# Moving read-outs, gates, norms and TensorE groups in the schedule of two state-space layers

## The chip, the core and the metric

The kernel runs on one core of a Trainium2 chip. That core has five engines which work side by side, each through its own instructions in order: TensorE (PE, matmuls; PEld is its weight load), VectorE (DVE), ScalarE (ACT), GpSimd (POOL) and SyncE (SP), which here only issues DMA transfers. They wait for one another by semaphores. The metric is the device time of one launch in microseconds (us), lower is better. Before the change the median of three runs is 9307.3 us (9303.51 to 9308.01).

## The reference

The network takes `x` of 8 images, 384 channels, 32 x 32 pixels, in float32, and applies four layers, each as `x = x + layer(group_norm(x))`:

- Layer 0 is a Mamba block over the 1024 pixels of an image as a sequence.
- Layer 1 is a deformable depthwise convolution with three kernel sizes.
- Layer 2 is a layer norm, the same state-space block, and an MLP with exact gelu.
- Layer 3 shifts channel groups and convolves them.

The change touches layers 0 and 2. Their common core, cut to what matters (768 inner channels `d`, 16 states `n`, sequence `t`):

```python
xz = t @ in_proj_w.T;  xm, z = split(xz)
u  = silu(causal_conv3(xm) + conv_b)
dt, B, C = split(u @ x_proj_w.T)
dt = softplus(dt @ dt_proj_w.T + dt_proj_b)
h[t] = exp(dt * A) * h[t-1] + (dt * u) * B[t]      # for every d and n
y[t] = sum_n h[t] * C[t] + u * D
out  = (y * silu(z)) @ out_proj_w.T
# layer 2 alone: out = gelu(out @ mlp_w1.T) @ mlp_w2.T, after a layer norm in front
```

## The kernel before

Each state-space layer is one call of `ssm_layer` (L205). The sequence of an image is cut into two halves of 512 tokens, so there are 16 **steps** a layer (8 images x 2 halves). Counting from 0, an even step is the first half of an image and an odd step the second. The 768 inner channels are six tiles `j` of 128.

A tile has 8 **units** `m`. A unit is one scan instruction: 128 partitions hold 32 channels x 4 states, and the free dimension holds two further states of 512 tokens each, so 128 x 1024 elements. A step has 6 x 8 = 48 units, which the code counts as slots `t` 0 to 47. For each unit:

- `decays` (L490, ACT): `da = exp(dt * A)`, two instructions, into one of two PSUM buffers, two units ahead.
- `inputs` (L498, POOL): `db = du * B`, three units ahead, with three buffers.
- `scan` (L508, DVE): the recurrence, one instruction over `da` and `db`.
- `with_c` (L522): `hs = h * C`, on POOL for some units (`GP_C`: those scan straight into `hs`) and on DVE for the others. There are seven `hs` buffers.
- `keep_last` (L517, ACT): in the first half the last state is kept for the second; `first_token`, `carry` and `add_carry` (L463 to L487) put it in there.
- `read_out` (L530, PE): after each four units, 8 matmuls (16 rows in the trace, since each float32 matmul shows as two passes) add `hs` over the states into `y`, a single PSUM buffer. In layer 0 the first of the two read-outs of a tile begins with a matmul that adds `u * D`.

After the second read-out of a tile `close` (L553, DVE) multiplies `y` by the gate `silu(z)`.

Everything else is hung into this row of units by `plan` (L652). It fills four lists, for ACT, DVE, POOL and PE, with one entry per slot; `put(q, t, fn, ...)` adds a function to slot `t`. The order on each of these four engines is exactly the order in which the loop at L782 emits it (`tc.manual_schedule`), so a wait of one instruction holds up all that follow on its engine. Within a unit the order is: ACT's list, scan and its product, `keep_last`, `decays` of two units ahead, DVE's list, `inputs` of three ahead, POOL's product, POOL's list, PE's list, and then the read-outs kept in `late`. Read-outs kept in `early` are emitted at the beginning of a unit. SP's transfers are ordered by the framework, not by hand.

What `plan` places, with the slots that the change touches:

- the gates: `fetch_in` and `z_proj` (L542, PE) and `gate` (L548, ACT). Silu, gelu and the pair exp/ln lie in different ACT tables, so each gate is a table load, the silu, and by `exp_ln` (L376) a load back;
- the softplus of tile `j + 2`: `dt_proj` (PE), `soft_exp` (ACT), `soft_rest` (DVE, writes `sp_e`), `soft_ln` (ACT), and then in layer 0 `soft_add` (L441, PE: three matmuls by the identity into `ps_sp`), `soft_take` (L446, ACT) and `soft_du` (L449, DVE), and in layer 2 `soft_sum` (L432, POOL). `spread` (L453, SP) writes `dt` and `du` to DRAM and reads them back spread over the partitions as `dtb` and `dub`;
- the next step's input: `norm_load`, in odd steps the group norm of the next image (`gn_...`), `norm_apply`, in layer 2 the layer norm (`ln_mean` to `ln_affine`), the six inner projections with their convolution (`inner`, `conv_last`, `conv`, `silu`), `x_proj`, `x_store`, `load_bc`;
- the previous step's output: `out_proj` (L564), `out_take`, and in layer 2 the MLP in three groups (`mlp_up`, `up_take`, `gelu`, `mlp_down`, `down_take`), whose weights come through a ring of three buffers `wm`.

All these matmuls share three PSUM banks (`mm`), used in turn.

## Time and profile before

| | us |
|---|---|
| median of the runs | 9307.3 |
| profiled execution | 9306.84 |
| its span | 9305.0 |
| layer 0, 75 to 2902 of the span | 2827 |
| layer 1, 2902 to 5863 | 2961 |
| layer 2, 5863 to 8996 | 3133 |
| rest (tail of the MLP, layer 3), 8996 to 9305 | 309 |
| one unit's scan on DVE, mean | 2.28 to 2.29 |
| its product on DVE (where it has one) | 1.225 |
| `db` product on POOL | 2.356 |
| `hs` product on POOL (where it has one) | 2.354 |
| one decay on ACT (two a unit) | 0.691 |
| ACT table load | 1.283 |
| gate (silu of 128 x 512) on ACT | 0.597 |
| gelu of 128 x 2048 on ACT | 1.910 |
| six 128 x 128 x 512 matmul passes on PE | 2.74 |

How to read it: the span is the time from the first to the last instruction of the profiled execution. A stretch of the span can be asked for alone, and then shows how long each engine was busy in it. The list of waits says which instruction (engine, tile, line) waited for which, with the sum in us, the number of times and the longest. A timeline row gives start, duration, engine, line, operation, tiles and shapes, and in brackets the idle time of that engine just before it and what ended it. In the timelines of this document, times are us from the start of the span.

### The profile page before, as it was taken

What the parts mean: (1) busy time and instruction counts of PE and PEld (TensorE: products, weight loads), DVE (VectorE), ACT (ScalarE), POOL (GpSimd) and SP (SyncE); (2) the same over time, 40 slices, a digit from 0 to 9 for tenths busy, and PEclk for the clock granted to TensorE, in tenths of its full rate; (3) what the DMA queues carried; (4) which work ended last, traced back from release to release, by engine and by line L of the source; (5) the groups of instructions that cost most, each with busy time, mean ns of one, the idle gap of its engine ahead of it and who ended that gap; (6) DMA issues with size and microseconds to landing.
All of it is one profiled execution on the core that took longest, in us unless ns stands there. A gap on an engine that the chain in (4) does not pass through costs nothing. (4 is left out here: it accounts for less than half of the span.)

```text
span 9305.0 us, 93009 instructions
## 1 busy us (share of the span) xinstructions
PE 7688.2 (83%) x29427; PEld 3852.5 (41%) x29452; DVE 7740.8 (83%) x8617; ACT 6580.6 (71%) x10531; POOL 5646.0 (61%) x3393
## 2 busy tenths in 40 slices
PE   6777777777775999999999997588888888888886
PEld 2222222222222777777777776133333333333333
DVE  6999999999995778778878877788989889898973
ACT  5677677677674778778878877677777777777750
POOL 6999999999995000000000000798989989899964
PEclk8888888888887999999999998798999899999988
DMA  4444544544443333333333333466656666565656
GB/s 126 119 117 112 122 118 114 123 115 113 120 110 88 77 82 86 90 84 88 89 80 88 89 83 86 115 152 150 150 146 148 156 158 153 145 147 147 162 147 112
DMA packets 785232, 1094.48 MB, mean 118 GB/s; under 512 B 274962, under 2 KB 427954, under 8 KB 752984
## 3 DMA queue, kind: packets, MB, share of 16 engines
q1 hardware_dynamic: 722628, 1077.98, 47.3%
q10 hardware_dynamic: 62100, 10.44, 0.7%
q8 instruction: 236, 3.87, 0.2%
q14 instruction: 268, 2.20, 0.1%
HBM read 917.84 MB, written 170.33 MB: 117 GB/s over the span
## 5 line engine op out<-in xcount | busy, mean ns | idle before, releaser
L502 POOL TENSOR_TENSOR db<-dub,bc 128x1024 f32<-128x1024 f32 x1536 | 3604.3, 2356 | 381.3 <-DVE hs L514 183.9
L494 ACT ACTIVATE da<-dtb,vec 128x512 f32<-128x512 f32 x3072 | 2118.6, 691 | 622.0 <-DVE hs L527 356.8
L514 DVE TENSOR_TENSOR_SCAN da<-da,db 128x1024 f32<-128x1024 f32 x912 | 2087.2, 2289 | 268.7 <-ACT da L494 205.5
L435 POOL TENSOR_TENSOR dt<-dt,sp_e 128x512 f32<-128x512 f32 x96 | 122.5, 1276 | 2893.2 <-DVE sp_e L427 2893.2
L1597 PE MATMUL wacc<-fsm,fxk 128*128 128x221 f32 (+34 forms) x10624 | 1657.0, 315 | 96.4 <-DVE fsm L1567 94.0
L537 PE MATMUL y<-hs,cols 128*32 128x512 f32 x6144 | 1170.6, 710 | 631.9 <-POOL hs L525 554.3
L1597 PEld LDWEIGHTS wacc<-fsm,fxk 128*128 128x128 f32 x10624 | 1570.3, 195 | 234.5 <-DVE fsm L1567 157.8
L514 DVE TENSOR_TENSOR_SCAN hs<-da,db 128x1024 f32<-128x1024 f32 x624 | 1423.3, 2281 | 90.9 <-POOL db L487 60.9
L525 POOL TENSOR_TENSOR hs<-hs,bc 128x1024 f32<-128x1024 f32 x624 | 1468.6, 2354 | 32.8 <-ACT st L520 32.8
L1567 DVE TENSOR_TENSOR fsm<-fhy,fhx 128x170 f32<-128x170 f32 (+42 forms) x3216 | 1172.9, 434 | 345.3 <-PE wacc L1597 318.4
L527 DVE TENSOR_TENSOR hs<-da,bc 128x1024 f32<-128x1024 f32 x912 | 1117.0, 1225 | 78.8 <-PE y L537 23.3
L1527 ACT ACTIVATE fhy<-fpyx,cell 128x416 f32<-128x416 f32 (+9 forms) x1280 | 645.5, 576 | 388.1 <-DVE fsm L1567 388.1
L537 PEld LDWEIGHTS y<-hs,cols 128*32 128x32 f32 x6144 | 219.7, 119 | 1472.9 <-POOL hs L525 800.5
L1550 DVE TENSOR_TENSOR fxk<-fxt,fwk 128x1024 f32<-128x1024 f32 (+1 forms) x688 | 789.0, 1185 | 10.2 <-ACT fxt L1329 10.2
L614 PE MATMUL ps_m<-hid,wm 128*128 128x512 f32 x1152 | 608.8, 686 | 145.8 <-ACT hid L609 91.0
L595 PE MATMUL ps_h<-t,wm 128*128 128x512 f32 x1152 | 524.7, 599 | 24.5 <-DVE sp_e L427 15.0
L1532 ACT ACTIVATE fhy<-fhy,cols 128x1344 f32<-128x1344 f32 (+10 forms) x368 | 530.8, 1442 | 12.0
L614 PEld LDWEIGHTS ps_m<-hid,wm 128*128 128x128 f32 x1152 | 247.4, 222 | 511.8 <-issue 291.6
L1238 PE MATMUL ps_off<-fxn,fow 128*98 128x465 f32 (+10 forms) x896 | 386.6, 579 | 0.0
L1514 ACT ACTIVATE fhx<-fpyx,cell 128x544 f32<-128x544 f32 (+8 forms) x640 | 380.0, 666 | 0.0
L595 PEld LDWEIGHTS ps_h<-t,wm 128*128 128x128 f32 x1152 | 214.0, 190 | 322.6 <-issue 276.1
L569 PE MATMUL ps_o<-u,wm 128*128 128x512 f32 x576 | 292.1, 655 | 64.1 <-DMA wm<-in_wout 38.8
(212 smaller groups left out, 9969.6 us busy)
## 6 DMA issues: line engine op xcount, KB each, us to landing
dtb<-dtd SPq DMA_DIRECT2D x768, 256.0 KB
dub<-dtd SPq DMA_DIRECT2D x768, 256.0 KB
fpyx<-fposd SPq DMA_DIRECT2D x640, 256.0 KB
wm<-in_w SPq DMA_DIRECT2D x96, 768.0 KB
bc<-bcd SPq DMA_DIRECT2D x256, 256.0 KB
x<-x SPq DMA_DIRECT2D x71, 768.0 KB
dtd<-dt SPq DMA_DIRECT2D x192, 256.0 KB
dtd<-du SPq DMA_DIRECT2D x192, 256.0 KB
```

The source lines that it names most:

```text
L494: nc.scalar.activation(da[:, i, :], s["dtb", j][:, k, :], AF.Exp, scale=na[:, j, n + i : n + i + 1])
L502: nc.gpsimd.tensor_tensor(db, du, s["bc"][p][:, 0], ALU.mult)
L514: nc.vector.tensor_tensor_scan(h1, da1, db1, 0.0, ALU.mult, ALU.add)
L525: nc.gpsimd.tensor_tensor(s["hs", m], s["hs", m], c, ALU.mult)
L527: nc.vector.tensor_tensor(hs_tile(s, m), s["da", m], c, ALU.mult)
L537: nc.tensor.matmul(s["y"][k * IP : (k + 1) * IP, :], sel, s["hs", p * NSUB + k][:, i, :], start=mlp and p == 0 and i == 0, stop=p == NQP - ...
L595: nc.tensor.matmul(ps, s["w1", q][:, k, f * P : (f + 1) * P], s["t"][:, k, :], start=(k == 0), stop=(k == G - 1))
L614: nc.tensor.matmul(ps, s["w2", q][:, f, o * P : (o + 1) * P], s["hid", q][:, f, :], start=(f == 0), stop=(f == 3))
L1527: nc.scalar.activation(hy[:, at : at + (yb - ya) * W], pyx[:, 0, ya * W : yb * W], AF.Abs, bias=bias)
L1550: nc.vector.tensor_tensor(t[:, :n], x, wk[:, j : j + 1, :].to_broadcast([P, n, P]), ALU.mult)
L1567: nc.vector.tensor_tensor(self.sub(sm, at, [(r * w, n), (w, r), (1, w)]), self.sub(hy, hy_at[by] + xa, [(r * W, n), (W, r), (1, w)]), self ...
L1597: nc.tensor.matmul(a[:, ya - 4 * o : yb - 4 * o, xa:xb], k, self.sub(sm, sm_at[by], [(w, yb - ya), (1, w)]), start=False, stop=False,)
```

## The change

Eight edits, all in `ssm_layer`, with no instruction added to the arithmetic:

1. `du` no longer has a tile of its own; it is written into `sp_e` (the tile that `soft_rest` wrote). `sz` gets two buffers in layer 2.
2. Read-outs: the first of a tile (units 0 to 3) goes from the end of slot 4 to the end of slot 5; the second (units 4 to 7) from the beginning of the next tile's first unit to the end of that unit, behind PE's list. `early` disappears.
3. `close` goes from slot 1 to slot 2 of the next tile.
4. In layer 0 `soft_du` goes from slot 6 to slot 7 of the tile.
5. In layer 2 the gates of tiles 0 and 1 share one table visit at slot 8, those of 2 and 3 one at slot 24; the others come at 31 and 47 (before: 7, 15, 23, 31, 39, 47). The z projections move with them. Layer 0 keeps its slots.
6. The group norm's last parts (`gn_sum`, `gn_rstd`) and `norm_apply` go one slot later, the parts of the layer norm one or two.
7. In layer 2 the first three inner projections, `x_proj` and `x_store` go one or two slots later.
8. In layer 2 the halves of `out_proj`, and the groups of `mlp_up`, `mlp_down` and gelu, get new slots (gelu 17, 33, 42 becomes 15, 33, 41).

```diff
-                s["du", j] = du = p1.tile([P, TS], F32, name="du")
+                s["du", j] = du = s["e"]
...
             def gate(s, j):
-                sz = s["sz"] = p1.tile([P, TS], F32, name="sz")
-                nc.scalar.activation(sz, s["ps_z"], AF.Silu)
+                sz = s["sz", j] = p1.tile([P, TS], F32, name="sz", bufs=2 if mlp else 1)
+                nc.scalar.activation(sz, s["ps_z", j], AF.Silu)
...
+            TG, TS2 = ((8, 8, 24, 24, 31, 47), (24, 31)) if mlp else ((7, 15, 23, 31, 39, 47), (23, 31))
+            TZ = (6, 7, 22, 23, 30, 45) if mlp else tuple(t - 1 for t in TG)
+            TI = (16, 17, 18, 24, 25, 26) if mlp else (15, 16, 17, 24, 25, 26)
...
-                    put(dve, t + 1, close, *((s, j - 1) if j else (prev, ND - 1)))
-                    tz = t + (6 if pe_sum or mlp and j == 0 else 5)
+                    put(dve, t + 2, close, *((s, j - 1) if j else (prev, ND - 1)))
+                    tz = TZ[j]
                     put(pe, tz - 2, fetch_in, s, ND + j)
                     put(pe, tz, z_proj, s, j)
-                    g = t + 7
-                    put(act, g, gate, s, j)
-                    if j in (2, 3):
-                        put(act, g, silu, nxt, 3 * (j - 2), 3 * (j - 1))
-                    put(act, g, exp_ln)
+                    put(act, TG[j], gate, s, j)
...
-                        put(dve, t + 6, soft_du, n, k)
+                        put(dve, t + 7, soft_du, n, k)
...
+                for i, t in enumerate(TS2):
+                    put(act, t, silu, nxt, 3 * i, 3 * i + 3)
+                for t in sorted({*TG, *TS2}):
+                    put(act, t, exp_ln)
...
-                    put(dve, 7, lambda n: n.update(gn_var=self.gn_sum(n["gn_grp"][0], n["gn_ps"])), nxt)
-                    put(act, 8, lambda n: n.update(gn=self.gn_rstd(n["gn_grp"][0], n["gn_var"])), nxt)
+                    put(dve, 8, lambda n: n.update(gn_var=self.gn_sum(n["gn_grp"][0], n["gn_ps"])), nxt)
+                    put(act, 9, lambda n: n.update(gn=self.gn_rstd(n["gn_grp"][0], n["gn_var"])), nxt)
...
-                put(act, 9, norm_apply, nxt)
+                put(act, 10, norm_apply, nxt)
                 if mlp:
                     put(pe, 10, ln_mean, nxt)
-                    put(dve, 11, ln_center, nxt)
-                    put(act, 12, ln_square, nxt)
-                    put(pe, 12, ln_var, nxt)
-                    put(act, 13, ln_rstd, nxt)
-                    put(dve, 13, ln_scale, nxt)
-                    put(act, 14, ln_affine, nxt)
-                for d, t in enumerate((15, 16, 17, 24, 25, 26)):
+                    put(dve, 12, ln_center, nxt)
+                    put(act, 13, ln_square, nxt)
+                    put(pe, 13, ln_var, nxt)
+                    put(act, 14, ln_rstd, nxt)
+                    put(dve, 15, ln_scale, nxt)
+                    put(act, 16, ln_affine, nxt)
+                for d, t in enumerate(TI):
...
-                put(pe, 32 if mlp and pe_sum else 30, x_proj, nxt, 0, ND // 2)
-                put(pe, 33 if mlp and pe_sum else 32, x_proj, nxt, ND // 2, ND)
-                put(act, 34 if mlp and pe_sum else 33, x_store, nxt)
+                put(pe, 32 if mlp else 30, x_proj, nxt, 0, ND // 2)
+                put(pe, 33 if mlp else 32, x_proj, nxt, ND // 2, ND)
+                put(act, 34 if mlp else 33, x_store, nxt)
...
-                for o, (t, e) in enumerate(((0, 1), (2, 3), (4, 5)) if mlp else ((8, 9), (10, 11), (12, 13))):
+                for o, (t, e) in enumerate(((0, 2), (1, 3), (4, 5)) if mlp else ((8, 9), (10, 11), (12, 13))):
...
-                    ups = ((7, 8, 9, 11), (23, 27, 28, 31), (38, 39, 40, 41)) if pe_sum else ((7, 8, 11, 14), (22, 23, 27, 28), (38, 39, 40, 41))
-                    downs = ((18, 19, 20), (34, 35, 36), (43, 44, 46))
-                    for q, g in enumerate((17, 33, 42)):
+                    ups = ((8, 9, 11, 12), (27, 28, 29, 31), (37, 38, 39, 40))
+                    downs = ((19, 20, 21), (34, 35, 36), (43, 44, 46))
+                    for q, g in enumerate((15, 33, 41)):
...
-                    for r in early.pop(i, ()):
-                        read_out(*r)
                     run(act[t])
...
                     for r in late.pop(i, ()):
                         read_out(*r)
                     if m % NSUB == NSUB - 1:
-                        (early if m == NU - 1 else late).setdefault(i + 1, []).append((s, j, m // NSUB))
+                        late.setdefault(i + (1 if m == NU - 1 else 2), []).append((s, j, m // NSUB))
```

## The prediction

> **What bounds the kernel now.** I first read busy time by stage, because the change touches only the two state-space layers. Two stretches lie wholly inside them (columns: length, then busy us and instructions of PE, weight loads, DVE, ACT and POOL, the granted clock, DMA share, GB/s).
>
> ```profile
> 100.00:2900.00 2800.00, 2106.06 (x6069) 673.96 (x6068) 2565.31 (x1781) 1972.09 (x3439) 2612.24 (x1527) 0.85 0.47 114
> 5900.00:8990.00 3090.00, 2593.58 (x7598) 961.82 (x7596) 2735.99 (x2000) 2319.51 (x3779) 2845.00 (x1754) 0.90 0.61 148
> ```
>
> DVE and POOL are each busy 92 to 93% in the first layer and 89 to 92% in the second. Both bound the kernel: POOL makes `db` for each scan, DVE scans, and `db` has three buffers, so neither gets far ahead. What can be won is idle time that both lose. I therefore read who waited for whom. In 200 to 2700 us (678 `db` products, 48 a step: 14.1 steps):
>
> ```profile
> PE y L537 <- POOL hs L525: 344.6, 91, 6.4
> ACT dt L447 <- PE ps_sp L444: 128.8, 50, 5.4
> DVE du L451 <- ACT dt L447: 76.3, 42, 4.2
> POOL db L502 <- DVE hs L514: 94.2, 71, 3.1
> ```
>
> In 6000 to 8900 us (709 products, 14.8 steps):
>
> ```profile
> DVE da L514 <- ACT da L494: 137.2, 91, 3.1
> DVE gn_var L177 <- PE gn_ps L155: 38.5, 7, 6.0
> DVE hs L527 <- PE y L537: 23.3, 6, 4.3
> DVE xn L332 <- ACT ps_var L327: 21.1, 14, 2.3
> ```
>
> The first list is a chain of order: a read-out on PE's queue stands waiting for a POOL product, `soft_add` (L444) stands behind it, then ACT's copy and DVE's `du`. The timeline of one even step of layer 0, slots 9 to 15, shows it:
>
> ```profile
> 1522.07 3.63 PE L537 MATMUL y<-hs,cols 128*32 128x512 f32 x12 [4.29 <-POOL hs L525]
> 1525.63 6.58 PE L569 MATMUL ps_o<-u,wout 128*128 128x512 f32 x12
> 1546.70 0.58 ACT L447 COPY dt<-ps_sp 128x512 f32<-128x512 f32 x1 [5.40 <-PE ps_sp L444]
> 1547.32 0.69 DVE L451 TENSOR_TENSOR du<-ps_sp,u 128x512 f32<-128x512 f32 x1 [3.52 <-ACT dt L447]
> 1550.30 2.36 POOL L502 TENSOR_TENSOR db<-dub,bc 128x1024 f32<-128x1024 f32 x1 [2.83 <-DVE da L514]
> ```
>
> An odd step of layer 2 (the next step opens a new image, so its group norm is made here) has the largest hole, at slots 4 to 8:
>
> ```profile
> 6866.62 4.42 PE L569 MATMUL ps_o<-u,wm 128*128 128x512 f32 x6 [5.02 <-DMA wm<-in_wout]
> 6872.91 1.23 DVE L527 TENSOR_TENSOR hs<-da,bc 128x1024 f32<-128x1024 f32 x1 [3.14 <-PE y L537]
> 6875.71 0.59 ACT L586 COPY t<-ps_o 128x512 f32<-128x512 f32 x1 [10.32 <-PE ps_o L569]
> 6877.19 0.22 POOL L477 TENSOR_TENSOR a<-a,st 128x16 f32<-128x16 f32 x1 [4.81 <-ACT a L468]
> 6880.18 0.16 DVE L177 TENSOR_TENSOR gn_var<-gn_ps,gn_grp 128x3 f32<-128x3 f32 x1 [6.04 <-PE gn_ps L155]
> ```
>
> **The change, part by part.** *Layer 0, even steps (8).* With the read-out of tiles 4 to 7 moved behind slot 8's output projection, that projection's six matmuls (2.7 us by L546's like row, six in 2.74) run inside the 4.29 us wait, and PE's queue is 2.6 us ahead. At slot 13 `soft_add` now precedes the read-out (1.0 + 1.9 us): `ps_sp` is done near 1541.2, not 1546.7. ACT's copy then waits for nothing, and `du`, a slot later, neither. What is late next is the gate of slot 15: PE still does a projection half (2.6), the read-out (2.9) and the gate's matmuls (2.7), to 1549.4; then gate 0.60, table 1.28, decays 1.4: slot 17's scan starts near 1552.5, today 1555.46. So -3.0 us, which POOL follows, since its 2.83 us wait there was for DVE. 8 x 3.0 = -24.
>
> *Layer 0, odd steps (8).* `du` waits 4.19 us at slot 6. `soft_add` before the read-out ends near 1338, not 1343. But the read-out (5.6 us here) then lies ahead of the gate's matmuls (2.7): 1346.3, plus 0.60, 1.28 and 1.4 gives slot 9's scan at 1349.6, today 1350.90: -1.3. POOL moves no sooner: from 1339.98, when it had waited 1.97 us for `dub`, it works without a gap. 8 x 1.3 = -10.
>
> *Layer 2, odd steps (8).* The projection weights land no sooner (6866.62). Both projection halves now run before the read-out: 4.4 + 2.8 + 1.9 puts slot 7's product at 6875.7 (today 6872.91), but frees ACT's copy at 6873.9, POOL's carry at 6875.7 and slot 8's scan at 6877.2 (today 6880.26): 3.1 ahead. Then two gates wait in one visit for two z projections: 6875.7 + 2.7 + 2.1 (group-norm matmuls) + 2.7 = 6883.2; gate and reload 1.9, decays 1.4, `gn_rstd` and a hidden copy 1.9, decays 1.4, `norm_apply` 3.1 with a copy, decays 1.4: slot 12's scan at 6894.3, with `ln_center` (three of 0.68) still to come; today 6895.8 with it done. The lead is gone. I take 0; ends -3 and +3 (a whole product group of 2.7 late).
>
> *Layer 2, gates and gelu.* Gates at 7, 15, 23, 31, 39, 47 become visits at 8, 24, 31, 47. A visit is two loads and a gate, 1.28 + 0.60 + 1.28 = 3.16 us of ACT; two fewer a step free 2 x 2.57 us of loads, on an engine busy 75%. At 15 gelu (1.28 + 1.91 + 1.28 = 4.47) replaces a gate visit, 1.3 longer ahead of slot 17's scan, while `ln_scale` two slots later loses its 21.1 / 14.8 = 1.4 us wait: 0. At 39 the visit leaves and gelu goes from 42 to 41:
>
> ```profile
> 7599.80 2.30 DVE L514 TENSOR_TENSOR_SCAN da<-da,db 128x1024 f32<-128x1024 f32 x1 [1.00 <-ACT da L494]
> 7613.23 2.30 DVE L514 TENSOR_TENSOR_SCAN da<-da,db 128x1024 f32<-128x1024 f32 x1 [2.77 <-ACT da L494]
> ```
>
> These 3.8 us become one: ACT needs decays 1.4, copy 0.7 with a like wait on PE, gelu 4.47, decays 1.4 = 8.7 against DVE's 2.3 + 1.2 + 2.2 + 1.4 (`close`) = 7.1: 1.6 left, -2.2 in even steps. In odd steps POOL shows no wait from slot 31 on, so DVE's wait is covered there: 0. 8 x 2.2 = -18.
>
> The Trainium skill, "ScalarE: Activation LUTs", section "What ACT_TABLE_LOAD costs", counts a switch as the 1283 ns load plus a drain of about 1380 ns. In this trace a load of 1.28 us began at 1346.19 and its gate at 1347.49, with no drain between. By the page the two visits saved free 10.6 us of ACT a step, by the rows 5.1; with ACT 75% busy neither enters the sum, and were ACT the bound, the page would make the gain 170 us and the rows 82.
>
> *Re-laid TensorE groups.* No group is placed at slots 14 and 15 any more. The nearest row is six `ln_var` matmuls after 6.22 us of waiting, 5.49 us at a granted clock of 0.50 (7481.5 to 7487), beside 2.84 for six z matmuls at 1.00 (7489.2 to 7492). The first inner projection can so be 2.7 us late; ACT's `conv_last` has `ln_affine` and decays ahead of it. Taken 0, ends 0 and +2.7 a step.
>
> ```profile
> 7481.68 5.49 PE L321 MATMUL ps_var<-sq,mean_w 128*128 128x512 f32 x6 [6.22 <-ACT sq L316]
> 7489.21 2.84 PE L546 MATMUL ps_z<-xn,winr 128*128 128x512 f32 x6
> ```
>
> The Trainium skill, "TensorE: Matmul & The Clock Gate", section "What's actually happening", speaks against such a hole: about 3.4 us idle puts the array at half clock for the next 3.4 us or so. By it every step's inner projection starts cold, +1.7 us of PE; if that reached DVE the sum would be 27 us worse.
>
> *Edits taken at 0, with their cover.* `du` in `sp_e`: the next `soft_rest` must wait for the copy of `du` to DRAM; its issue lies 13 us or more ahead (7470.07 to 7483.45), and that cover ends only if SP is held longer. The transfers of `spread` leave with POOL's slot 7 as before; in odd layer-0 steps they stand on SP behind the residual load (1325.37), so a later `du` is hidden; else it costs a unit, 3.7 us x 8 = +30, or saves the 1.97. The z weights fetched at slot 5 rather than 11 pass `spread` on SP, 0.4 us of issue. `close` one slot later still lies three before the next use of `y`. `x_store` at 34 falls behind gelu of 33, so `dt_proj` may hold PE up to 3 us; the read-out of slot 37 is next, with PE busy 84%.
>
> Sum: -24 - 10 + 0 - 18 = -52. The profiled execution took 9306.84 us around a span of 9305.0, the median of three runs is 9307.3: 9255.
>
> **Rivals.**
> *All named waits convert* (20%): layer 0's `du` wait, 76.3 / 14.1 = 5.4 a step, x 16 = 87; layer 2's `gn_var`, `hs` and `xn` waits, 82.9 / 14.8 = 5.6, x 16 = 90. That gives 9130. For: ACT's copies are freed as well. Against: POOL is gapless in odd steps.
> *Absorbed* (13%): DVE's gains meet a POOL that was the bound anyway, and only a lead of about 1 us in the eight even steps of layer 0 is left; 9300. For: 92 to 93% on POOL. Against: its wait of 2.83 is for DVE.
> *Slower* (20%): ACT becomes the bound in layer 2's slots 8 to 17, where two gates, norms, gelu and `ln_affine` are now packed. Uncovered, gelu costs 4.47 x 16 = 72 against layer 0's 34: 9345. It decides from 3.3 us a step (52 / 16). For: DVE already waits for decays, 137.2 us. Against: one gate visit and `ln_scale`'s wait leave the same place.
>
> **How the numbers follow.** Forecast 47%. Low end 9165, part of the way to the first rival; high end 9350, the slower rival; a tenth is left out on each side. The forecast's own range is 9215 to 9309 (layer 2's odd steps 24 either way, `dub` -16 or +30). 0.2% (19 us) is about what a measurement tells from no change; faster 0.67 (forecast and first rival), same 0.13, slower 0.20.
>
> **What would show it.** Right: `du`'s wait for ACT and ACT's for `ps_sp` nearly gone, slot 17's scan 3 us sooner, `gn_var`'s wait gone, two fewer gate loads a step (88 to about 59 in the same window). Wrong: DVE's wait for decays in layer 2 above 137 us, `ps_in` or `y` as new waits, or `dub` later.

## The result, and the profile after

The changed kernel takes 9296.95 us (median of 14 runs, 9289.11 to 9301.38), the kernel before 9304.54 (14 runs beside it, 9293.37 to 9310.48): a ratio of 0.9991, 95% interval 0.9983 to 0.9999. That is 7.6 us faster, inside the 0.2% which the prediction called no change; it had said 9255. The profiled execution after took 9297.33 us around a span of 9295.5. From the start of a layer's first scan to the end of its last scan the two traces give:

| | before, us | after, us | difference | forecast |
|---|---|---|---|---|
| layer 0 | 2826.5 | 2804.0 | -22.5 | -34 |
| layers between (no edit) | 2961.5 | 2956.4 | -5.1 | 0 |
| layer 2 | 3132.8 | 3148.2 | +15.4 | -18 |
| after it (no edit) | 308.9 | 311.4 | +2.5 | 0 |

So layer 0 won two thirds of its part, and layer 2 lost instead of winning. The same order of layer 0 was run again in e1, e7 and e8 below and took 2801.2, 2807.5 and 2804.2 us, the old order of layer 2 took 3130.3 in e1. Each layer time is read from one profiled execution, and these four of one order span 6.3 us, so differences of under 7 us between two layers are not read as anything, and those of 8 to 13 us stand only a little above that.

The two stretches inside the state-space layers, with the columns as in the prediction:

```profile
100.00:2900.00 2800.00, 2025.35 (x6126) 691.60 (x6117) 2564.61 (x1786) 1980.56 (x3439) 2612.61 (x1527) 0.81 0.47 114
5900.00:8990.00 3090.00, 2568.70 (x7618) 957.68 (x7619) 2721.28 (x1994) 2217.26 (x3687) 2819.41 (x1741) 0.90 0.61 148
```

In the second, ACT is busy 102 us less than before (2217.26 against 2319.51), and the layer is longer all the same: what the fewer loads on ACT gave was lost elsewhere. Who waited for whom in 200 to 2700 us, after (total us, times, longest; a tile of the name `sp_e` now holds `du` too):

```profile
PE ps_sp L444 <- ACT dt L414: 239.2, 51, 7.9
PE ps_sp L444 <- DVE sp_e L425: 226.8, 64, 5.6
PE y L537 <- POOL hs L525: 37.8, 26, 3.3
ACT sz L550 <- PE ps_z L546: 73.4, 70, 1.9
ACT dt L447 <- PE ps_sp L444: 10.1, 13, 1.3
DVE da L514 <- POOL db L502: 38.2, 19, 2.5
DVE da L514 <- POOL db L487: 33.6, 22, 3.4
```

The chain shown before the change is gone: the read-out's wait for POOL fell from 344.6 to 37.8 us, the copy's wait for `ps_sp` from 128.8 to 10.1, and `du` is on DVE's list no more (76.3). In their place PE waits 466 us ahead of the `soft_add` for its inputs, the gate waits 73.4 us for its product (before 14.9, at the gate of slot 15 alone; now at most of a step's six gates), and the scans wait for POOL (38.2 + 33.6 us).

And in 6000 to 8900 us:

```profile
DVE da L514 <- ACT da L494: 84.5, 47, 2.6
DVE hs L514 <- ACT da L494: 43.5, 28, 2.4
DVE hs L527 <- PE y L537: 52.1, 22, 6.6
DVE y L556 <- PE y L537: 24.4, 14, 2.0
DVE gn_var L177 <- PE gn_ps L155: 7.9, 7, 1.1
ACT hid L606 <- PE ps_h L595: 152.6, 98, 5.1
PE ps_dt L408 <- ACT dbc L391: 50.3, 14, 3.9
```

`gn_var`'s wait went from 38.5 to 7.9, the scans' waits for decays from 137.2 to 84.5 + 43.5. DVE waits longer for PE, 52.1 us (before 23.3) for read-outs ahead of its products and, newly, 24.4 at the closing of slot 18, and ACT waits 152.6 us (before 63.7) for the hidden tiles of the MLP: PE is late.

### The profile page after: what moved, and what is told of

The parts are those of the page before. It is cut to its first block, busy times and chain, and to the rows that moved or that the text cites. A ratio compares the mean times of both kernels' runs of the same rounds, so it can differ in the third digit from the quotient of the medians.

```text
span 9295.5 us, 93074 instructions
## 1 busy us (share of the span) xinstructions
PE 7557.6 (81%) x29452; PEld 3856.6 (41%) x29452; DVE 7733.3 (83%) x8617; ACT 6500.3 (70%) x10467; POOL 5645.4 (61%) x3393
## 5 line engine op out<-in xcount | busy, mean ns | idle before, releaser
L525 POOL TENSOR_TENSOR hs<-hs,bc 128x1024 f32<-128x1024 f32 x624 | 1470.8, 2357 | 15.2 <-ACT st L520 14.9
L537 PE MATMUL y<-hs,cols 128*32 128x512 f32 x6144 | 826.1, 618 | 160.5 <-POOL hs L525 154.6
L1551 DVE TENSOR_TENSOR fxk<-fxt,fwk 128x1024 f32<-128x1024 f32 (+1 forms) x688 | 787.1, 1179 | 10.2 <-ACT fxt L1330 10.2
L614 PE MATMUL ps_m<-hid,wm 128*128 128x512 f32 x1152 | 550.2, 633 | 61.7 <-ACT hid L609 27.7
L537 PEld LDWEIGHTS y<-hs,cols 128*32 128x32 f32 x6144 | 171.3, 112 | 798.3 <-issue 497.7
L348 PE MATMUL ps_in<-xn,winr 128*128 128x512 f32 x576 | 328.9, 718 | 174.5 <-ACT xn L337 125.4
L444 PE MATMUL ps_sp<-dt,ident 128*128 128x512 f32 x192 | 168.4, 974 | 290.8 <-ACT dt L414 285.7
L614 PEld LDWEIGHTS ps_m<-hid,wm 128*128 128x128 f32 x1152 | 226.9, 203 | 394.3 <-issue 282.7
L444 PE MATMUL ps_sp<-sp_e,ident 128*128 128x512 f32 x192 | 174.9, 1009 | 259.5 <-DVE sp_e L425 259.5
```

Source lines behind the costliest of these rows:

```text
L525: nc.gpsimd.tensor_tensor(s["hs", m], s["hs", m], c, ALU.mult)
L537: nc.tensor.matmul(s["y"][k * IP : (k + 1) * IP, :], sel, s["hs", p * NSUB + k][:, i, :], start=mlp and p == 0 and i == 0, stop=p == NQP - ...
L614: nc.tensor.matmul(ps, s["w2", q][:, f, o * P : (o + 1) * P], s["hid", q][:, f, :], start=(f == 0), stop=(f == 3))
L1551: nc.vector.tensor_tensor(t[:, :n], x, wk[:, j : j + 1, :].to_broadcast([P, n, P]), ALU.mult)
```

## The experiments

The layers run one after the other, so each kernel tries one thing in layer 0 and another in layer 2; the durations of both layers are read from its trace. The edits are shown against the changed kernel; `...` stands for lines of an edit that are left out, and the heading or the expectation says what they do. "First" and "second" read-out mean those after units 3 and 7 of a tile. Where a read-out goes back to its place of before, `early` and the loop that empties it are as they were. The ratios are to runs of the kernel before on the same chip, whose median lay between 9293 and 9305 us.

| kernel | layer 0, us | layer 2, us | median, us | ratio to before (95%) |
|---|---|---|---|---|
| before | 2826.5 | 3132.8 | | |
| after | 2804.0 | 3148.2 | 9296.95 | 0.9991 (0.9983 to 0.9999) |
| e1 | 2801.2 | 3130.3 | 9281.54 | 0.9977 (0.9968 to 0.9987) |
| e2 | 2804.0 | 3215.8 | 9369.10 | 1.0074 (1.0057 to 1.0091) |
| e3 | 2822.6 | 3122.3 | 9289.51 | 0.9987 (0.9977 to 0.9997) |
| e4 | 2808.8 | 3284.5 | 9439.90 | 1.0150 (1.0133 to 1.0167) |
| e5 | 2782.6 | 3115.9 | 9243.19 | 0.9937 (0.9921 to 0.9954) |
| e6 | 2837.2 | 3146.8 | 9325.54 | 1.0024 (1.0014 to 1.0034) |
| e7 | 2807.5 | 3123.8 | 9272.83 | 0.9968 (0.9957 to 0.9979) |
| e8 | 2804.2 | 3124.7 | 9275.61 | 0.9972 (0.9962 to 0.9981) |
| e9 | 2783.1 | 3125.8 | 9257.67 | 0.9961 (0.9947 to 0.9975) |
| e10 | 2783.1 | 3143.0 | 9273.81 | 0.9979 (0.9969 to 0.9988) |
| e11 | 2818.0 | 3148.7 | 9312.28 | 1.0018 (1.0008 to 1.0027) |
| e12 | 2855.5 | 3144.7 | 9349.71 | 1.0062 (1.0045 to 1.0079) |
| e13 | 2782.9 | 3143.4 | 9269.86 | 0.9967 (0.9955 to 0.9980) |
| e14 | 2782.8 | 3155.2 | 9281.61 | 0.9981 (0.9971 to 0.9991) |
| e15 | 2780.6 | 3128.4 | 9257.56 | 0.9957 (0.9940 to 0.9974) |

**e1: the second layer in its old order.**

```diff
-            TG, TS2 = ((8, 8, 24, 24, 31, 47), (24, 31)) if mlp else ((7, 15, 23, 31, 39, 47), (23, 31))
+            TG, TS2 = (7, 15, 23, 31, 39, 47), (23, 31)
...
-                    ups = ((8, 9, 11, 12), (27, 28, 29, 31), (37, 38, 39, 40))
+                    ups = ((7, 8, 11, 14), (22, 23, 27, 28), (38, 39, 40, 41))
```

> First state-space layer as after the change, second one re-laid as before it (du stays in the buffer of sp_e in both). In the traces the first layer lasted 2826.5 us before the change and 2804.0 after it, the second 3132.8 and 3148.2, from the first to the last scan of each. Theory (the first layer's moves win about 22 us, the re-laying of the second loses about 15): the second layer lasts 3130 to 3136 and the whole run about 9282 us, 22 below the kernel before. Rival (the second layer lost its 15 us to du in the buffer of sp_e or to the place that each tile has on the chip, not to the order of its work): the second layer lasts 3145 to 3150 again and the whole stays at 9297.

9281.54 us, layer 2 back at 3130.3. The order of the work in layer 2 loses the 15 us; `du` in the buffer of `sp_e`, which stayed, costs nothing that shows.

**e2: layer 0 with read-outs and closing alone; layer 2 with these at their old places.**

```diff
-                    put(dve, t + 2, close, *((s, j - 1) if j else (prev, ND - 1)))
+                    put(dve, t + (1 if mlp else 2), close, *((s, j - 1) if j else (prev, ND - 1)))
-                        put(dve, t + 7, soft_du, n, k)
+                        put(dve, t + 6, soft_du, n, k)
...
-                        late.setdefault(i + (1 if m == NU - 1 else 2), []).append((s, j, m // NSUB))
+                        q = early if mlp and m == NU - 1 else late
+                        q.setdefault(i + (1 if mlp or m == NU - 1 else 2), []).append((s, j, m // NSUB))
...
```

> Two halves that do not touch each other. First layer: only the read-outs and the closing of y are moved, while du stays at slot 6 and the norms at 7 to 9. Theory of the prediction (the read-out ahead of the soft_add is what made du late): the first layer lasts 2802 to 2808 us, all of the 22 won. Rival (du's own move to slot 7 is what wins): 2822 to 2828. Second layer: as after the change, except that read-outs and closing are where they were before it. Theory (the closing at slot 18 waits 2 us a step for a read-out that now stands behind the inner projection, and PE falls late by the read-outs that come later): the second layer lasts about 3116 us, 32 less than the 3148 after the change. Rival (the read-outs' new place costs nothing on balance, since gn_var's 6 us wait comes back with the old one): 3148 or more.

In layer 0 the theory held: 2804.0, all of the gain from read-outs and closing, none from `du` or the norms. In layer 2 it fell. The rival's side held, with 3215.8, 67.6 us more, but not for its reason: `gn_var` does not wait again; the scans wait 188.3 us for decays in 6000 to 8900 us, where they waited 128.0 after the change. Among the new groups the late read-outs were needed.

**e3: layer 0 with `du` alone; layer 2 with the third MLP group and the x projection back.**

```diff
-                put(pe, 32 if mlp else 30, x_proj, nxt, 0, ND // 2)
-                put(pe, 33 if mlp else 32, x_proj, nxt, ND // 2, ND)
-                put(act, 34 if mlp else 33, x_store, nxt)
+                put(pe, 30, x_proj, nxt, 0, ND // 2)
+                put(pe, 32, x_proj, nxt, ND // 2, ND)
+                put(act, 33, x_store, nxt)
-                    ups = ((8, 9, 11, 12), (27, 28, 29, 31), (37, 38, 39, 40))
+                    ups = ((8, 9, 11, 12), (27, 28, 29, 31), (38, 39, 40, 41))
-                    for q, g in enumerate((15, 33, 41)):
+                    for q, g in enumerate((15, 33, 42)):
...
```

> Two halves that do not touch each other. First layer: only du is moved to slot 7, read-outs, closing and norms stay as before the change. Theory (the read-out's place wins): 2815 to 2828 us, at most half of the 22 won, since ACT's own copy of the sum still waits for PE; rival (du's move wins): 2802 to 2808. Second layer: as after the change, with the third group of the MLP's up products at slots 38 to 41 again, its gelu at 42 and the x projection at 30, 32 and 33. Theory (after the change PE is late from slot 34 to 41: gelu waits 5.0, 2.3 and 0.9 us a step for its hidden tile, and the scans of slots 41 and 43 wait 1.6 and 2.6 us for their decays because of it): the layer lasts about 3123 us, 25 less than after the change. Rival (those waits are taken out of slack that the scans have anyway): 3145 to 3150.

Both theories held: layer 0 2822.6, layer 2 3122.3, 25.9 us less. The timeline of one even step of layer 2 after the change, slots 34 to 43 (start, us, engine, line, work, idle time ahead and what ended it):

```profile
7164.84 2.07 PE L408 MATMUL ps_dt<-dbc,wdt 24*128 24x512 f32 x2 [3.88 <-ACT dbc L391]
7181.99 0.69 ACT L606 ACTIVATE hid<-ps_h,vec 128x512 f32<-128x512 f32 x1 [5.01 <-PE ps_h L595]
7186.62 0.69 ACT L606 ACTIVATE hid<-ps_h,vec 128x512 f32<-128x512 f32 x1 [2.33 <-PE ps_h L595]
7188.89 2.30 DVE L514 TENSOR_TENSOR_SCAN da<-da,db 128x1024 f32<-128x1024 f32 x1 [1.65 <-ACT da L494]
7198.70 2.30 DVE L514 TENSOR_TENSOR_SCAN da<-da,db 128x1024 f32<-128x1024 f32 x1 [2.61 <-ACT da L494]
```

and of the same step in e3, slots 34 to 44:

```profile
7170.95 1.12 PE L411 MATMUL ps_dt<-dbc,wdt 24*128 24x512 f32 x2
7176.02 2.30 DVE L517 TENSOR_TENSOR_SCAN da<-da,db 128x1024 f32<-128x1024 f32 x1 [2.75 <-ACT da L497]
7192.25 0.67 ACT L609 ACTIVATE hid<-ps_h,vec 128x512 f32<-128x512 f32 x1
7208.72 2.30 DVE L517 TENSOR_TENSOR_SCAN da<-da,db 128x1024 f32<-128x1024 f32 x1 [1.36 <-ACT da L497]
```

After the change the store of the x projection stands behind the gelu of slot 33. PE waits 3.88 us for it, with the down products queued behind, and these are followed at once by the third group's up products. So ACT stands still for 7.3 us ahead of two hidden tiles, has their copies and the gelu close together, and two scans, of slots 41 and 43, find their decays late by 4.3 us. In e3 PE does not wait there; its scans are late at slot 35 (2.75 us, after the change 0.97) and slot 44 (1.4). From the scan of slot 34 to that of slot 44 a step takes 42.1 to 42.4 us after the change and 39.1 in e3, in even and odd steps alike (means of six steps each). Even steps win this back in other slots, 191.4 us against 191.2; the odd ones do not, 204.6 against 201.3, and there the layer loses. Why only they lose was not tried.

**e4: layer 0 with the gate's product a slot earlier; layer 2 with each gate on a visit of its own.**

```diff
-            TG, TS2 = ((8, 8, 24, 24, 31, 47), (24, 31)) if mlp else ((7, 15, 23, 31, 39, 47), (23, 31))
-            TZ = (6, 7, 22, 23, 30, 45) if mlp else tuple(t - 1 for t in TG)
+            TG, TS2 = (7, 15, 23, 31, 39, 47), (23, 31)
+            TZ = (6, 13, 21, 29, 37, 45) if mlp else tuple(t - 2 for t in TG)
```

> Two halves that do not touch each other. First layer: as after the change, with each gate's product a slot earlier, so that the gate on ACT does not wait for it (it waits 1.2 to 1.8 us at slots 7, 16, 24 and 40). Theory (these waits on ACT are what gives the scans of slots 9, 17 and 41 their 1.3 to 1.8 us): the first layer lasts about 2780 us, 24 less. Rival (ACT's waits are cover for something else, the scans then wait for POOL or DVE): 2800 to 2808. Second layer: as after the change, but each tile's gate again on its own visit, at slots 7, 15, 23, 31, 39 and 47, with six loads of the table more a step. Theory (two gates in one visit save what the two loads cost on ACT, 1.28 us each): the second layer is longer by 0 to 25 us, 3148 to 3173. Rival (a double visit of ACT, two gates and a silu of three tiles behind each other, makes the decays behind it late by more than the two loads cost): 3125 to 3140.

In layer 0 the rival's side held: 2808.8. In layer 2 every figure was far too small: 3284.5, 136 us more. ACT in slots 15 and 16, and the scan that waits for the decays behind it:

```profile
7133.84 1.28 ACT L553 ACT_TABLE_LOAD   x1
7135.14 0.60 ACT L553 ACTIVATE sz<-ps_z 128x512 f32<-128x512 f32 x1
7137.03 1.28 ACT L612 ACT_TABLE_LOAD   x1
7138.32 1.91 ACT L612 ACTIVATE hid<-hid 128x2048 f32<-128x2048 f32 x1
7143.24 2.30 DVE L517 TENSOR_TENSOR_SCAN da<-da,db 128x1024 f32<-128x1024 f32 x1 [5.26 <-issue]
```

The change moved a gelu to slot 15, where a gate had its visit. With both there, ACT does 7.7 us without decays, and DVE is out of work for 5.3 us (the profile names no releaser; ACT's decays end at 7143.15, 0.1 us before). The pairing of the gates is what makes room for the gelu of slot 15. Slots 15 and 16 are 6.0 us longer in even steps and 6.7 in odd ones, of about 10 us a step, and slot 39, where a gate is back, 2.6 and 2.5: in that order the pairing is worth 136 us.

**e5: layer 0 with the second read-out and the closing alone; layer 2 as before the change with the gates paired.**

```diff
-                        late.setdefault(i + (1 if m == NU - 1 else 2), []).append((s, j, m // NSUB))
+                        late.setdefault(i + 1, []).append((s, j, m // NSUB))
 # layer 2: all but the gates and z projections at its slots of before
...
```

> Two halves that do not touch each other. First layer: as after the change, but of each tile's two read-outs only the second one moves (a slot's place later, with the closing at two); the first stays at its old place, ahead of the soft_add. Theory (the first read-out ahead of the soft_add is what made du late): the layer lasts 2820 to 2828 us, nothing won. Rival (the second one, ahead of the products of the next tile's first slots, is what held): 2801 to 2808. Second layer: as before the change (3132.8 us), but gates of two tiles in one visit, with their products placed as after the change. Theory (a part of the re-laying that wins by itself, six table loads of 1.28 us a step on ACT): 3110 to 3130. Rival (it pays only together with the earlier gelu, which without it collides with the gate of slot 15): 3130 to 3145.

Layer 0: 2782.6, 43.9 us under before and 21.4 under after. The prediction's theory fell; the rival's side held, beyond its range. Layer 2: 3115.9, so the pairing wins 16.9 us by itself. The whole is the fastest kernel of this study: 9243.19 us, 0.9937 of before. Its waits in 200 to 2700 us (`du` is now called `sp_e`, L454):

```profile
PE y L540 <- POOL hs L528: 266.1, 89, 6.4
PE ps_sp L447 <- DVE sp_e L428: 20.0, 21, 1.3
ACT dt L450 <- PE ps_sp L447: 99.9, 45, 4.9
ACT sz L553 <- PE ps_z L549: 10.5, 14, 1.6
DVE sp_e L454 <- ACT dt L450: 1.0, 1, 1.0
```

The wait that headed the list before the change is mostly still there (266.1 of 344.6 us), and the layer is 43.9 us shorter; after the change, which leaves 37.8 of it, the layer is longer by 21.4. So the wait itself was not the price. Sorted by slot it was 217 us at the first read-out and 127 at the second before, and is 135 and 131 in e5: the second read-out waits as long as ever, but now behind PE's list of its slot, so that what the list has there, in slot 8 an output projection's first half, no longer stands behind it.

**e6: layer 0 with the first read-out alone; layer 2 as before with late read-outs and closing.**

```diff
-                    put(dve, t + 2, close, *((s, j - 1) if j else (prev, ND - 1)))
+                    put(dve, t + (2 if mlp else 1), close, *((s, j - 1) if j else (prev, ND - 1)))
-                        late.setdefault(i + (1 if m == NU - 1 else 2), []).append((s, j, m // NSUB))
+                        q = early if not mlp and m == NU - 1 else late
+                        q.setdefault(i + (1 if m == NU - 1 else 2), []).append((s, j, m // NSUB))
 # layer 2: everything else at its slots of before
...
```

> Two halves that do not touch each other. First layer: as after the change, but of each tile's two read-outs only the first one moves, and the closing stays a slot after the tile. Theory (the first read-out ahead of the soft_add is what made du late): all of the 22 us won, 2801 to 2808. Rival: 2820 to 2828. Second layer: as before the change, but read-outs and closing placed as after it. Theory (the late read-outs win in the second layer too, as putting them back there cost 67 us): 3060 to 3090. Rival (they win only with the groups of TensorE that the change laid out round them): 3125 to 3145.

Layer 0: 2837.2, 10.7 us worse than before and beyond the rival's range too. Layer 2: 3146.8, 14 worse, the rival's side. PE and ACT in an even step of layer 0 after the change (slots 11 to 15):

```profile
1527.62 1.13 PE L444 MATMUL ps_sp<-dt,ident 128*128 128x512 f32 x2
1532.88 1.02 PE L534 MATMUL y<-u,diag_d 128*128 128x512 f32 x2
1533.83 1.92 PE L537 MATMUL y<-hs,cols 128*32 128x512 f32 x16
1535.68 2.84 PE L546 MATMUL ps_z<-xn,win 128*128 128x512 f32 x6
1538.56 0.60 ACT L550 ACTIVATE sz<-ps_z 128x512 f32<-128x512 f32 x1 [1.60 <-PE ps_z L546]
```

and in e5:

```profile
1515.58 1.02 PE L537 MATMUL y<-u,diag_d 128*128 128x512 f32 x2
1516.53 1.93 PE L540 MATMUL y<-hs,cols 128*32 128x512 f32 x16
1518.38 1.13 PE L447 MATMUL ps_sp<-dt,ident 128*128 128x512 f32 x2
1523.64 2.74 PE L549 MATMUL ps_z<-xn,win 128*128 128x512 f32 x6
1526.41 0.60 ACT L553 ACTIVATE sz<-ps_z 128x512 f32<-128x512 f32 x1 [0.83 <-PE ps_z L549]
```

In e5 the first read-out comes ahead of the `soft_add`; after the change it comes between that and the gate's product, 2.9 us of work, and the gate waits twice as long. In the stretch shown the scans still lose next to nothing by it. They lose at other gates: slots 15 and 24 of odd steps take 6.1 and 5.5 us after the change and 4.8 and 4.3 in e5, slot 40 of even steps 4.1 and 2.7. PE also stands before the `soft_add` for `sp_e` or `dt`, as the list of after showed. TensorE's granted clock falls too, from 0.85 in e5 to 0.81 (100 to 2850 us), but the 95 products of gates there take 270 us instead of 260, against 63 us more of gates' waits in 200 to 2700 us, so the clock is at most a small part of these.

**e7: layer 2 as in e3, with the third out projection's weights fetched ahead of x.**

```diff
+                if mlp:
+                    put(pe, 0, fetch, prev, "out", 2)
                 put(pe, 0, norm_load, nxt)
```

> First layer as after the change (2801 to 2804 us). Second layer as after the change with the third group of the MLP back at its old slots (this gave 3122.3 us), and one thing more: the load of the third out projection's weights is put on SP's queue ahead of the next step's loads of x, behind which it stood some 8 us in every second step. Theory (that load, landing late, makes PE and so the scan of slot 7 late in odd steps, 9.5 to 9.9 us for a scan of 3.5): the odd steps are 4 to 6 us shorter, the layer 3075 to 3090. Rival (slot 7 waits for the sums of the norm, which come from the very loads of x that are now one load later): no gain, or up to 8 us more, 3120 to 3130.

3123.8, the rival. Layer 0 is as after the change. The odd steps after the change had this hole, in slots 4 to 8:

```profile
6849.84 7.16 PE L569 MATMUL ps_o<-u,wm 128*128 128x512 f32 x12 [5.46 <-DMA wm<-in_wout]
6858.87 1.23 DVE L527 TENSOR_TENSOR hs<-da,bc 128x1024 f32<-128x1024 f32 x1 [6.33 <-PE y L537]
6863.56 0.16 DVE L177 TENSOR_TENSOR gn_var<-gn_ps,gn_grp 128x3 f32<-128x3 f32 x1 [1.12 <-PE gn_ps L155]
```

and e7 this one, at slot 3:

```profile
6837.22 1.88 DVE L295 BATCH_NORM_STATS2 gn_st<-x 128x6 f32<-128x512 f32 x3 [7.00 <-DMA x<-x]
6843.19 7.14 PE L572 MATMUL ps_o<-u,wm 128*128 128x512 f32 x12
6852.20 1.23 DVE L530 TENSOR_TENSOR hs<-da,bc 128x1024 f32<-128x1024 f32 x1 [0.71 <-PE y L540]
```

Against e3, from scan to scan, slot 7 of odd steps went from 9.5 to 4.4 us and slot 3 from 7.3 to 12.3. Whichever of the two loads is second makes a hole of the same size. In both kernels the eight transfers that read `dtb` and `dub` back are issued between the two, and what needs the load behind them starts 10.2 us (weights, issued at 6839.66) or 10.4 us (`x`, issued at 6826.78) after its issue. Whether these eight are the reason was not tried.

**e8: layer 2 as before, with gates paired and both read-outs late.**

```diff
 # layer 2: norms, inner and out projections, MLP groups at their slots of before
-                    put(dve, 15, ln_scale, nxt)
+                    put(dve, 13, ln_scale, nxt)
...
```

> First layer as after the change (2801 to 2804 us). Second layer as before the change, with the gates of two tiles in one visit and the late read-outs and closing, but norms, inner projections, out projections and the MLP's groups at their old slots. Theory (these two parts win, and the re-laid groups of TensorE and later norms are what loses): about 3050 to 3100 us, the whole near 9220. Rival (each needs the re-laid groups): 3130 or more.

3124.7: neither. The two do not add up to a gain like e2's, and the late read-outs cost 8.8 us on top of the paired gates.

**e9: e5, and in layer 2 the second read-out and the closing late as well.** (Shown against e5.)

```diff
-                    put(dve, t + (1 if mlp else 2), close, *((s, j - 1) if j else (prev, ND - 1)))
+                    put(dve, t + 2, close, *((s, j - 1) if j else (prev, ND - 1)))
...
```

> First layer: only the second read-out of a tile and the closing are later (this gave 2782.6 us). Second layer: as before the change, with the gates of two tiles in one visit (this alone gave 3115.9 us) and, again, only the second read-out and the closing later. Theory (in both layers the second read-out wins and the first one loses, since behind the soft_add or the products of its slot it holds the gate's product up): the second layer lasts 3085 to 3105 us and the whole run 9212 to 9232. Rival (in the second layer the place of the read-outs costs whichever of them moves, as both together gave 14 us more there): 3116 to 3135, the whole 9243 to 9262.

Layer 2 took 3125.8, the rival: in its old groups the move of the second read-out and the closing costs 9.9 us, while in layer 0 it wins.

**e10: layer 0 as in e5 with `du` at 6; the third group's up products back in layer 2, the x projection not.**

```diff
-                        put(dve, t + 7, soft_du, n, k)
+                        put(dve, t + 6, soft_du, n, k)
-                    ups = ((8, 9, 11, 12), (27, 28, 29, 31), (37, 38, 39, 40))
+                    ups = ((8, 9, 11, 12), (27, 28, 29, 31), (38, 39, 40, 41))
-                    for q, g in enumerate((15, 33, 41)):
+                    for q, g in enumerate((15, 33, 42)):
...
```

> First layer: only the second read-out and the closing later, and du at slot 6 again instead of 7. Theory (the first read-out still holds the soft_add up at its old place, and du at 7 is what covers that): du waits for ACT again and the layer lasts 2795 to 2812 us instead of 2782.6. Rival (the second read-out's move frees PE so much that the soft_add is in time): 2780 to 2785. Second layer: as after the change, with the third group's up products at slots 38 to 41 and its gelu at 42 again, but the x projection and its store left at 32 to 34. Theory (the up products, which now stand right behind the down products of the second group, are what makes gelu and decays late): 3120 to 3130 us, all of the 26 won. Rival (the store of the x projection, behind the gelu of slot 33, is what holds PE, as the prediction feared): 3140 to 3150, nothing won.

Layer 0: 2783.1, the rival's time, but not its reason: `du` does wait again, 54.3 us for ACT in 200 to 2700 us, where it waited 1.0 in e5. That costs nothing in the sum: even steps take 170.0 us instead of 170.9, odd ones 178.6 instead of 177.4. Layer 2: 3143.0, 5.2 of 25.9 us won, the rival again. Seen from e3, the x projection's later slots alone cost 20.7 us.

**e11: layer 0 with the closing alone; layer 2 as in e3 with the first read-out at its old place.**

```diff
-                        late.setdefault(i + (1 if m == NU - 1 else 2), []).append((s, j, m // NSUB))
+                        q = early if not mlp and m == NU - 1 else late
+                        q.setdefault(i + 1, []).append((s, j, m // NSUB))
...
```

> First layer: as after the change, but both read-outs at their old places; only the closing is a slot later. Theory (the second read-out's place wins, by letting the output projection run while PE would wait for POOL): 2818 to 2828 us, at most a third of the 44 won. Rival (the later closing is what wins, as DVE no longer stands in for y): 2780 to 2790. Second layer: as after the change, with the third group back and the first read-out at its old place, the second one and the closing late. Theory (the first read-out's move loses here as in the first layer): 3095 to 3112 us, against 3122.3 with both moved. Rival: 3120 or more.

Layer 0: 2818.0, 8.5 of the 43.9 us, as the theory had it: with the closing late, the second read-out's place wins the other 35.4. (Whether it would without the later closing was not tried.) Layer 2: 3148.7 against e3's 3122.3, the rival: among the new groups the first read-out's move wins 26 us (among the old ones 1.1, e9 to e8), where in layer 0 it loses 21. The two layers want opposite things.

**e12: the fetch of e7 and a norm two slots later; the gate's product a slot earlier in layer 0.**

```diff
-                    put(dve, 3, norm_stats, nxt, 1)
+                    put(dve, 5 if mlp else 3, norm_stats, nxt, 1)
...
-                    put(act, 16, ln_affine, nxt)
+                    put(act, 18, ln_affine, nxt)
...
```

> First layer: only the second read-out and the closing later, and each gate's product a slot earlier. Second layer: as e9_best_of_both, with the third output projection's weights fetched ahead of the loads of x and the whole chain of the norm two slots later (statistics at slot 5, sums at 10, layer norm from 12 to 18, the first inner projections at 19 to 21, the first gelu at 15). Theory (the hole of odd steps is a matter of two loads of which the second one is always late, and it goes if what needs the second one stands two slots later): slot 3 and slot 7 of odd steps both fall under 6 us, and the layer is 30 to 60 us under that of e9. Rival (the time comes back where norms, inner projections and MLP groups now crowd, slots 16 to 26): the same as e9 or more.

Besides what the expectation names, the first MLP group stands at other slots than in e9 (up products at 8, 9, 11 and 12, down products from 16). Both named slots fell as expected, to 3.5 and 4.2 us, but slot 10 of the odd steps rose to 10.2 and slots 14 and 16 to 5.9 and 6.3; the layer took 3144.7, 18.9 more than e9. The hole moves to where the norm now stands. Layer 0 took 2855.5, 73 more than e5: a slot earlier, the gate's product stands in front of the `soft_add`, and the copy's wait for it rises from 99.9 us to 195.3 in 200 to 2700 us.

**e13: layer 0 as in e5; only the x projection back in layer 2.**

```diff
-                put(act, 34 if mlp else 33, x_store, nxt)
+                put(act, 33, x_store, nxt)
...
```

> First layer: only the second read-out and the closing later (2782.6 us). Second layer: as after the change, except that the x projection and its store stand at slots 30, 32 and 33 again; the third group's up products stay at 37 to 40, its gelu at 41. Theory (the store, which falls behind the gelu of slot 33, holds the dt projection and all that is queued behind it on PE): most of the 26 us won, the layer 3122 to 3130. Rival (the two parts lose together, either put back alone gives a few us): 3140 to 3146, as with the up products put back alone (3143.0).

(The two projections went back to 30 and 32 with it.) 3143.4, the rival. Together with e10: either part put back alone wins 5 us, which is no more than profiles of one order differ by, and both win 26. Seen from e3, each of the two alone costs 21 us: one is enough to use up PE's lead.

**e14: layer 2 as in e3, with the norms and first inner projections back too; e15: e5, with these as after the change in layer 2.**

```diff
-            TI = (16, 17, 18, 24, 25, 26) if mlp else (15, 16, 17, 24, 25, 26)
+            TI = (15, 16, 17, 24, 25, 26)
-                put(act, 10, norm_apply, nxt)
+                put(act, 9, norm_apply, nxt)
...
```

> First layer: second read-out and closing later, norms at their old slots 7 to 9 (2780 to 2786 us by every theory, as du's slot did not matter there either). Second layer: as after the change with the third group and x projection back (3122.3 us), and the norms, the layer norm and the first inner projections back at their old slots as well. Theory (the later norms win what gn_var waited, 6 us in every second step, and the MLP's first two groups lose it again): 3140 to 3175. Rival (neither does anything): 3118 to 3128.

> First layer: second read-out and closing later (2782 us). Second layer: as before the change, with the gates of two tiles in one visit (3115.9 us) and the norms, layer norm and first inner projections a slot or two later; read-outs, closing and the MLP's groups as before the change. Theory (the later norms win gn_var's wait of 6 us in every second step): 3070 to 3100, and the whole run near 9210. Rival (the wait is only passed on, to the scans behind it, since the sum that gn_var needs comes late whatever stands ahead): 3110 to 3125, the whole near 9243.

e14: 3155.2, so among the new groups the later norms win 33 us. e15: 3128.4, past the rival's range, so among the old ones they lose 12.5. The small sum of norms and first MLP groups, -2.4 us from e8 to e3, is +30.5 and -32.9.

## Why the prediction was wrong

*The sum.* -52 was forecast; traced, the two layers gave -7.1. Against the forecasts of its four terms the profiles give -19.8 for layer 0's even steps (-24), -2.7 for its odd steps (-10), -2.7 for layer 2's even steps (-18) and +18.1 for its odd steps (0). Every sign of being right that the prediction named came, or nearly: `du` and ACT's copy hardly wait, the scan of slot 17 in layer 0's even steps comes 3.1 us sooner after the step's start, `gn_var`'s wait falls to 7.9 us, the gates' loads to 59. What it named was reached, and the time was lost mostly where it had put no price.

*Layer 0.* In the middle of the layer even steps fell from 175.3 to 172.1 us on average; odd ones stayed, 179.1 and 179.5. The chain of order was read rightly, and its first half, the second read-out behind the output projection, wins more than was given it: with the closing, 43.9 us. The step that failed is "`soft_add` now precedes the read-out", counted as a gain. It takes 21.4 us back. Its cost was in the working ("the read-out (5.6 us here) then lies ahead of the gate's matmuls"), but at one gate a step, where the trace has most of the six wait, 73.4 us instead of 14.9; and it was set against a gain in `du` that was not there: e5 keeps the copy's wait of 99.9 us, and in e10 `du` waits 54.3 us without making the layer longer. (The even step's terms also add up to a scan at 1552.7, not 1552.5, -2.8 us instead of -3.0, which changes little.)

*Layer 2, gates.* "-2.2 in even steps", 8 x 2.2 = 18 us, stands for the pairing: alone it gave -16.9, its even steps took mostly 189 to 190 us instead of 191 to 193, and the gain lies where it was placed, 2.5 us in slots 39 to 43 of even steps. The loads of the gates' table fell as forecast, from 88 to 59 (after, groups of ACT in 6000 to 8900 us):

```profile
L550 ACT ACT_TABLE_LOAD x59 | 75.7, 1283 | 1.0
```

But e5 has its gelu at 42, and the prediction worked the term out with gelu at 41 and a wait on PE of about 0.7 us ahead of a hidden tile. In the change whole ACT waits 5.01 and 2.33 us there, and slots 39 to 43 of even steps take 21.5 us, where they took 20.3 before and 17.8 in e5. The term was also added to other moves as if each had a price of its own. Along one path of kernels the layer went 3132.8 (before), 3115.9 (gates, e5), 3124.7 (read-outs and closing, e8), 3155.2 (out projections and first two MLP groups, e14), 3122.3 (norms and inner projections, e3), 3148.2 (third group and x projection, after): -17, +9, +30, -33, +26. Undone from the other end the same parts had other prices: the gates 136 instead of 17, the read-outs a gain of 68 instead of a loss of 14. In the change whole, the first two steps of the layer, in which its work starts up, carry +10.4 of its +15.4.

*The edit taken at 0.* "`x_store` at 34 falls behind gelu of 33, so `dt_proj` may hold PE up to 3 us; the read-out of slot 37 is next, with PE busy 84%." This is the step that failed in layer 2. The wait is there, 3.88 us. Its cover was named by an average: what is next is a row of down and up products without a gap. Against e3 this edit alone costs 20.7 us (e10), the third group a slot earlier alone 21.1 (e13), both 25.9, and without them the layer is 10.5 us under before. It should have had a range like the others.

*Layer 2, odd steps.* Slot 7 lasts 9.9 us instead of 13.5 and `gn_var`'s wait falls as said, and the steps are 204.6 us against 202.5 on average, inside the ends of -3 and +3. But "the lead is gone" did not hold where it was said: at the scan of slot 12 it is 3.4 us (1.5 was worked out, with 2.0 us of `ln_center` still to come), at slot 18 5.6. It goes in slots 18 to 23 (4.4 us) and, after 1.3 won back, in 34 to 42 (6.2 us, of which slot 43 gives 2.1 back), where the x projection and the third MLP group stand. That these steps end near the 0 was luck. The projection weights, late as before, make the hole of slot 7; e7 and e12 show that it moves with the order of the loads and does not close.

*Empty slots 14 and 15.* The cold group came, and it is read at the granted clock, the last of the three times below being DVE's wait for the read-out behind it:

```profile
7087.71 5.13 PE L348 MATMUL ps_in<-xn,winr 128*128 128x512 f32 x6 [8.01 <-ACT xn L337]
7094.62 2.84 PE L348 MATMUL ps_in<-xn,winr 128*128 128x512 f32 x6
7094.79 0.76 DVE L556 SCALAR_TENSOR_TENSOR y<-u,vec,y 128x512 f32<-128x512 f32 x1 [1.94 <-PE y L537]
```

The clock was 0.54 in the first group and 1.00 in the second, after 8.01 us of idle time, and the group took 2.3 us more. The Trainium skill, "TensorE: Matmul & The Clock Gate", section "What's actually happening", has an array that was idle for a window of about 3.4 us at half clock, and this trace agrees. The prediction's estimate from that page was 1.7 us; the 2.3 measured decide. The prediction's cover for it (`ln_affine` and decays ahead of ACT) left out the read-out and the closing of slot 18, which waits 1.4 to 2.0 us a step. What that alone costs the layer was not tried.

*Table loads.* The Trainium skill, "ScalarE: Activation LUTs", section "What ACT_TABLE_LOAD costs", adds a drain of about 1380 ns to a switch. In e4 the gate starts 20 ns after its load ends (7133.84 + 1.28, then 7135.14), so no run here shows the drain. Neither price explains the pairing: two visits' loads are 5.1 us a step, and the pairing was worth 1.1 us a step in one order and 8.5 in the other.

*Rivals.* The slower rival, ACT as the bound in slots 8 to 17, did not come: its sign, DVE's wait for decays above 137 us, stood at 128 (84.5 + 43.5). Two other signs of being wrong did come: `y` as a new wait (24.4 us at slot 18), and ACT's wait for `ps_in` doubled, from 42.7 to 84.0 us. e4 shows the same mechanism, in the place named, when the gates are not paired. "Absorbed" gives the nearest time (9300), but not for its reason: it left layer 0 a gain of 8 us, and layer 0 gained 22.5 and layer 2 lost 15.4.

## What to carry to other kernels

A long wait in a list is worth something only if what is queued behind it is late. Here two read-outs waited for the same engine: moving the one with the smaller share won 35 us (44 with the closing), and moving the other as well lost 21, though it took nearly all of the wait away. In an order written by hand, moves have no price of their own: try each alone and each left out, and add prices only along a path that was run. A cover given as an average busy share is no cover; look at what stands in the next two slots.

## What was not expected of the hardware

Two gate visits fewer took 5.1 us of table loads a step off ACT and made a step 1.1 us shorter, but the same 2.56 us a visit, put next to a gelu (7.7 us of ACT in a row), stop the scans for 5.3 us. And of two loads on SP's queue, the weights of a projection and an input tile, with the eight transfers of `dtb` and `dub` between them, the second made a hole of about 5 us, in either order.
